# One pool for each PSUM bank, and a new order of the steps behind the attention of layer 0, in a two-layer float32 network

## The chip, the cores and the metric

The kernel runs on one core of one Trainium2 chip. The metric is the device time of one execution in microseconds (us): the median of several executions. All arithmetic is in float32; the score matmuls take their operands as pairs of rounded and residual parts.

## What is computed

The input is two images of 256 channels and 64 x 64 pixels. Cut to what matters here, the reference is:

```
# layer 0: attention over all 4096 pixels, 8 heads of 32 channels
xn  = group_norm(x)                       # groups of 8 channels
q, k, v = 1x1 convolutions of xn, with bias
x1  = x + softmax(q.T k / sqrt(32)) v

# layer 1, on n = group_norm(x1)
q, k, v = 1x1 convolutions of n           # w1, w2, w3
ctx   = attention among the 64 pixels of equal place in their 8 x 8 blocks
feats = relu(scale * (lr @ ctx) + shift)
qx, kx = two (1x1 convolution, relu) steps each of feats     # fq1 fq2, fk1 fk2
ctx2  = attention inside each 8 x 8 block; values fv @ feats
att   = relu(scale * (srw @ ctx2) + shift)
conv  = 3x3 grouped convolution of nine mixtures of q, k, v
out   = x1 + rate1 * att + rate2 * conv
```

Normalisation in layer 1 needs the mean and the variance of x1 for each group, and so every output of layer 0.

## The kernel before, in words

Channels are two chunks of 128 partitions (index k), pixels eight tiles of 512 (index t). The two images (index b) are worked one after the other, each in four stages, and each stage has its own division of PSUM, which has eight banks of 512 float32 per partition.

1. *Projections of layer 0* (project0, L408), pool ps0_b of eight banks. Each tile of q and k is evicted twice, by ACT (rounded part, L421) and DVE (residual, L422). For image 0, fold_scores (L196) makes products of the weights of layer 1 that turn its first attention into a product with one matrix g.
2. *Attention of layer 0* (attention0, L473), pool sc_b: a ring of seven banks in one tile for scores (L504), and one bank for the sums of values, av (L577). TensorE writes scores into the ring (L545), ACT takes Exp from it into a ring of 28 tiles in SBUF named es and v (L551), TensorE multiplies these with the values (L560), and DVE and DMA add them for the softmax denominators. Sixteen groups of heads and pixels are worked so. The denominators ("rows") of all but the last group go through DRAM. For the last group they are summed by TensorE into one bank of the ring, in two halves (sum_rows, L621), ahead of the last three blocks of values.
3. *First attention of layer 1* (layer1_first, L1147), pool ps1_b of eight banks. to_groups (L1154) normalises a tile into the tile xg, regrouped by place in the block. project (L1172) multiplies with g (tile py), then come the small attentions, one for each t (group_attention, L1047), whose last product pc_lr ACT evicts into feats (L1142).
4. *Second attention and convolution* (layer1_second, L1284): four banks for the convolution (pacc_b) and a pool ps2_b of four for the rest.

Between 2 and 3 stands finish_last (L660): it takes reciprocals of the rows (L674), copies the rows for a later check (kept, L680 for image 0 and L683 for image 1), multiplies the sums with the reciprocals, adds bias and input (L685), takes statistics of the result (L687 to L691), and gives back put, which copies the last 32 channels into the x tiles (L695), one copy for each of four tiles. At the start of stage 3 follow, for the second chunk, statistics over groups (Stats: means, spread, variances, deviations), with two tiny matmuls (pm_l, pv_l).

In stage 3, image 0 also has fold_products (L249). It transposes w3 and fv (tiles pt_w and pt_fv, copied by ACT at L259), and multiplies them with lr and srw (pm_w and pm_fv, copied at L267), so that two products of the network become one. It is a generator: each next(fold) issues one step, between steps of to_groups.

**What sets the order.** The framework records instructions and a planner orders those of each engine by simulated readiness. Inside tc.manual_schedule the named engines keep the written order: TensorE, ACT and DVE in attention0 and at the start of layer1_first (L1212), TensorE alone later. ACT and DVE work of stage 4, and in the kernel before the POOL work of stage 3, is ordered by the planner, which may also let the tail of one hand-ordered part overlap the head of the next. A tile of a pool that follows another pool in the same place waits until the tiles it covers are released. Accesses to one bank of one tile are kept in order across engines, unless tc.declare_no_dep says otherwise. xg is in the same place of SBUF as most of the ring es (pool apool, tag A), so that nothing may be written to xg before the last matmul has read es.

In the kernel before, the eight tiles of to_groups for the first chunk go to POOL (t = 5, 6, 7) and to ACT (the rest), and those of the second chunk to ACT (two for image 0, three for image 1) and DVE.

## Time and profile before

| what | us |
|---|---|
| median of 3 executions (3056.49 to 3058.67) | 3057.96 |
| the profiled execution, its own time | 3062.01 |
| its span, from the first to the last instruction | 3060.1 |
| TensorE (PE) busy in the span | 2979.3 |
| VectorE (DVE) busy | 2455.9 |
| ScalarE (ACT) busy | 2340.2 |
| GpSimd (POOL) busy | 832.1 |

The stages of image 0 meet at about 113 us (projections to attention), 1136 us (attention to layer 1) and 1248 us (first to second attention of layer 1); those of image 1 at about 1637, 2662 and 2764 us. The mean granted TensorE clock was 0.991.

A profile row names line, engine, operation, tile written <- tiles read, shapes, count, then busy time in us, mean duration in ns, and the engine's idle time before these instructions with what ended it. PEld is the loading of weights into TensorE. In the list of waits, a row is the waiting engine and line, the releasing one, the total in us, how often, and the longest. Buffer numbers and what follows them are cut from names: xg_0 is xg, pm_l1_0 is pm_l, wt_w3 is wt_w.

### The profile page before, as it was taken

The numbers are of one execution on the slowest core, as the hardware profiler recorded it, in microseconds if no ns is written. First come the engines' busy times: TensorE is split into PE (matmuls) and PEld (weight loads), VectorE is DVE, ScalarE is ACT, GpSimd is POOL, SyncE is SP. The second block draws the span as 40 slices with busy tenths as digits, with TensorE's granted clock in tenths as the row PEclk, the third lists the DMA queues.
The fourth block names the chain that finished last, engine by engine and source line by source line (L and its number), as shares of the span: only waits on it lengthen the run. The fifth ranks groups of instructions, "written<-read, shape, count | busy, mean of one in ns | idle before, by whom it ended". The sixth has DMA issues, their size and how long they took to land. (4 is left out here: it accounts for less than half of the span.)

```text
span 3060.1 us, 63941 instructions
## 1 busy us (share of the span) xinstructions
PE 2979.3 (97%) x25129; PEld 1859.9 (61%) x25129; DVE 2455.9 (80%) x3122; ACT 2340.2 (76%) x3266; POOL 832.1 (27%) x918
## 2 busy tenths in 40 slices
PE   7999999999999999999989999999999999999998
PEld 4565556655556556577755555666555565576765
DVE  4598998989899999856556989989988899835543
ACT  2699999999999984623237999999999999834333
POOL 1022222322223230155301222222222222306440
PEclk9999999999999999999999999999999999999999
DMA  7978789787897661230159787797878976700000
GB/s 259 274 137 180 150 163 175 153 172 157 176 181 159 140 135 42 73 131 28 42 193 274 134 169 163 159 181 146 174 162 167 183 160 131 170 5 4 21 15 22
DMA packets 244149, 425.01 MB, mean 139 GB/s; under 512 B 98889, under 2 KB 109949, under 8 KB 241661
## 3 DMA queue, kind: packets, MB, share of 16 engines
q0 software_dynamic: 94720, 237.57, 40.2%
q1 hardware_dynamic: 148972, 182.99, 21.6%
q8 instruction: 199, 3.26, 0.4%
q14 instruction: 114, 0.93, 0.1%
q10 hardware_dynamic: 144, 0.26, 0.0%
HBM read 119.55 MB, written 68.39 MB: 61 GB/s over the span
## 5 line engine op out<-in xcount | busy, mean ns | idle before, releaser
L551 ACT ACTIVATE es<-ring 128x512 f32<-128x512 f32 (+2 forms) x1572 | 1203.1, 904 | 29.9 <-PE ring L545 21.7
L545 PE MATMUL ring<-q,k 128*128 128x512 f32 x4096 | 1081.8, 407 | 11.2 <-ACT v L551 4.9
L597 DVE TENSOR_TENSOR e<-e,es 128x1024 f32<-128x1024 f32 (+1 forms) x956 | 1036.2, 1148 | 22.5 <-ACT es L551 22.2
L545 PEld LDWEIGHTS ring<-q,k 128*128 128x128 f32 x4096 | 733.4, 188 | 379.7 <-ACT es L551 115.7
L551 ACT ACTIVATE v<-ring 128x512 f32<-128x512 f32 (+2 forms) x1024 | 780.4, 899 | 23.8 <-PE ring L545 13.4
L560 PE MATMUL av<-es,v 128*32 128x256 f32 (+1 forms) x9684 | 725.2, 389 | 0.0
L597 DVE TENSOR_TENSOR e<-e,v 128x1024 f32<-128x1024 f32 (+1 forms) x636 | 670.1, 1112 | 22.4 <-ACT v L551 21.5
L560 PE MATMUL av<-v 128*32 128x256 f32 (+1 forms) x6188 | 498.0, 389 | 0.0
L560 PEld LDWEIGHTS av<-es,v 128*32 128x32 f32 x9684 | 328.3, 109 | 265.3 <-issue 105.5
L560 PEld LDWEIGHTS av<-v 128*32 128x32 f32 x6188 | 221.2, 109 | 171.2 <-issue 72.8
L996 PE MATMUL mm<-v,wf 128*128 128x256 f32 x1024 | 227.6, 380 | 1.5 <-DVE z L1005 1.5
L607 POOL DMA_DIRECT2D es<-es x118 | 100.7, 853 | 461.6 <-ACT es L551 411.4
L996 PEld LDWEIGHTS mm<-v,wf 128*128 128x128 f32 x1024 | 193.3, 190 | 36.8 <-issue 9.8
L986 POOL TENSOR_TENSOR v<-col 128x512 f32<-128x512 f32 x128 | 165.7, 1319 | 178.4 <-ACT rk_sr L1142 38.7
L1001 ACT COPY z<-mm 128x512 f32<-128x512 f32 x32 | 18.7, 586 | 183.3 <-PE mm L996 183.3
L607 POOL DMA_DIRECT2D acc<-es x118 | 119.5, 1018 | 113.8 <-ACT v L551 35.2
L605 POOL DMA_DIRECT2D es<-es x20 | 11.4, 569 | 495.2 <-ACT es L551 404.6
L607 POOL DMA_DIRECT2D es<-v x72 | 61.3, 852 | 290.8 <-ACT v L551 287.2
L1002 DVE TENSOR_TENSOR z<-z,mm 128x512 f32<-128x512 f32 x32 | 22.0, 687 | 140.1 <-ACT z L1001 139.7
L607 POOL DMA_DIRECT2D v<-es x112 | 114.3, 1020 | 17.7 <-ACT es L551 8.4
L607 POOL DMA_DIRECT2D acc<-v x78 | 75.1, 963 | 76.0 <-ACT es L551 31.1
L982 POOL TENSOR_TENSOR col<-xp 128x1152 f32<-128x1152 f32 x32 | 69.6, 2174 | 66.5 <-DVE xp L1420 55.1
(254 smaller groups left out, 2665.5 us busy)
## 6 DMA issues: line engine op xcount, KB each, us to landing
acc<-es POOLq DMA_DIRECT2D x128, 512.0 KB, 6.4
acc<-v POOLq DMA_DIRECT2D x84, 512.0 KB, 6.2
es<-es POOLq DMA_DIRECT2D x138, 256.0 KB, 4.3
v<-es POOLq DMA_DIRECT2D x132, 256.0 KB, 5.1
k<-wk_halves SPq DMA_DIRECT2D x64, 512.0 KB
q<-wq_halves SPq DMA_DIRECT2D x256, 128.0 KB
v<-v POOLq DMA_DIRECT2D x90, 256.0 KB, 5.0
es<-v POOLq DMA_DIRECT2D x84, 256.0 KB, 3.9
```

Of the source, the lines that this page charges most:

```text
L545: touch(nc.tensor.matmul(sc[:, i, :], held["k", g // 2][:, j * P : (j + 1) * P], held["q", g, u // 2][:, u % 2, :], start=True, stop=True, ...
L551: nc.scalar.activation(dst, sc, AF.Exp, scale=SC0), set(range(at % BANKS, at % BANKS + m))
L560: note(nc.tensor.matmul(dst[HD0 * u : HD0 * u + HD0, n], lhs, rhs(u)[:, n], start=start, stop=stop))
L597: nc.vector.tensor_add(dst[:, s, :], dst[:, s, :], src)
L605: nc.gpsimd.dma_start(out=dst, in_=src)
L607: nc.gpsimd.dma_start(out=dst, in_=src, accum_op=ALU.add)
L982: (nc.gpsimd.tensor_add if plus else nc.gpsimd.tensor_sub)(col, cols(one), cols(two))
L986: (nc.gpsimd.tensor_add if plus else nc.gpsimd.tensor_sub)(dst, rows(one), rows(two))
L996: nc.tensor.matmul(mm[:, m, r, :], wf[:, k, 4 * r + q, m * P : (m + 1) * P], v[r // 2][:, r % 2, k, :], start=k == 0, stop=k == KC - 1,)
L1001: nc.scalar.copy(z[:, 1], mm[:, :, 1, :])
L1002: nc.vector.tensor_add(z[:, 0], z[:, 1], mm[:, :, 0, :])
```

## The change

There are five parts.

1. *Banks.* Instead of one pool with four or eight buffers, open_banks opens one pool for each bank; bank() hands them out in strict turn, or one by number. av gets a pool of its own. Named banks: the second g product of fold_scores and the last q tile of image 1 take bank 7; the last pc_lr tiles take banks 2 and 3.
2. *Rows of the last group.* The two halves lie in two banks of the ring. The reciprocal and the kept copy are made half by half, with no dependence on the matmuls of the other half. For image 0, DVE multiplies the sums straight from PSUM; the ACT copy of them is gone.
3. *Folds.* Both transposes come first and then the four products, one step each.
4. *to_groups* walks its tile in the order of the input: reads have step 1, stores have step 64 elements (256 bytes) in runs of eight; before, it was reads of step 8 and stores of step 1 in runs of eight.
5. *Order of stage 3.* POOL is ordered by hand too. First chunk: image 0 has six tiles on ACT and two on POOL, image 1 seven on ACT and one on POOL. The copies of put are placed between POOL's tiles.

```diff
-    def bank(shape, name):
-        return psum["ps"].tile(shape, F32, tag="bank", name=name)
+    def open_banks(name, first):
+        stack = ExitStack()
+        places = range(first, 8)
+        psum.update(
+            turn=0, first=first,
+            banks={i: stack.enter_context(tc.tile_pool(name=f"{name}_{i}", bufs=1, space=PSUM)) for i in places},
+        )
+        return stack
+
+    def bank(shape, name, at=None):
+        if at is None:
+            at = psum["first"] + psum["turn"] % len(psum["banks"])
+            psum["turn"] += 1
+        return psum["banks"][at].tile(shape, F32, tag="bank", name=name)
...
-            pg = bank([P, C + AT], f"pt_g_{k}")
+            pg = bank([P, C + AT], f"pt_g_{k}", at=7 if k else None)
...
-        for name, behind in (("w3", "lr"), ("fv", "srw")):
-            turned = w4([P, KC, C], "turned_" + name)
+        turned = {}
+        for name in ("w3", "fv"):
+            turned[name] = w4([P, KC, C], "turned_" + name)
             for j in range(KC):
...
-                nc.scalar.copy(turned[:, j, :], pt)
+                nc.scalar.copy(turned[name][:, j, :], pt)
             yield
+        for name, behind in (("w3", "lr"), ("fv", "srw")):
             for k in range(KC):
...
                 nc.scalar.copy(wts[name][:, k, :], pt)
+                yield
             nc.sync.dma_start(out=kept_w[name], in_=wts[name])
-            yield
...
-                pq = bank([P, T], f"p_{nt}")
+                final = b > 0 and (nm, g, t) == ("wq0", KC - 1, NT - 1)
+                pq = bank([P, T], f"p_{nt}", at=7 if final else None)
...
-                sums[g] = psum["sc"].tile([P, T], F32, tag="av", name=f"av_{b}_{g}")
+                sums[g] = psum["av"].tile([P, T], F32, tag="av", name=f"av_{b}_{g}")
...
                 for part in range(2):
+                    at, note = rows[part], rows_made[part].append
                     for j in SUMMED_LAST:
-                        quarters(rows, ones, lambda u: unit(g, j, u), j == SUMMED_LAST[0], False, part)
+                        quarters(ring[:, at, :], ones, lambda u: unit(g, j, u), j == SUMMED_LAST[0], False, part, note)
...
-            for part in range(2):
-                n = slice(part * T // 2, (part + 1) * T // 2)
-                nc.vector.reciprocal(avs[:, 1, n], rows[:, n])
             kept = w4([P, T], f"kept_{b}")
             y = avs[:, 0, :]
-            if b == 0:
-
-                nc.scalar.copy(y, sums[g])
-                nc.scalar.copy(kept, rows)
-                nc.vector.tensor_mul(y, y, avs[:, 1, :])
-            else:
-                nc.scalar.copy(kept, rows)
-                nc.vector.tensor_mul(y, sums[g], avs[:, 1, :])
+            for part, at in enumerate(rows):
+                n = slice(part * T // 2, (part + 1) * T // 2)
+                for made in (nc.vector.reciprocal(avs[:, 1, n], ring[:, at, n]), nc.scalar.copy(kept[:, n], ring[:, at, n])):
+                    for other in rows_made[1 - part]:
+                        tc.declare_no_dep(made.ins, other.ins, reason="another bank of the ring")
+            nc.vector.tensor_mul(y, sums[g], avs[:, 1, :])
...
-                    held["rows"] = spare_bank()
+                    held["rows"] = []
+                    for _ in range(2):
+                        spare_bank()
+                        held["rows"].append(spare[0])
...
-            pc = bank([P, T], f"pc_{nm}_{m}")
+            pc = bank([P, T], f"pc_{nm}_{m}", at=ends and ends[m])
...
-            dst = xg[:, k, :, t, :].rearrange("p (d e) o -> p d e o", d=8)
-            src = xts[t][:, k, :].rearrange("p (d o e) -> p d e o", d=8, o=8)
+            dst = xg[:, k, :, t, :].rearrange("p (d e) o -> p d o e", d=8)
+            src = xts[t][:, k, :].rearrange("p (d o e) -> p d o e", d=8, o=8)
...
-        with tc.manual_schedule(engines={E.PE, E.Activation, E.DVE}):
+        with tc.manual_schedule(engines={E.PE, E.Activation, E.DVE, E.Pool}):
             st.aggregate(second)
             fold = fold_products() if b == 0 else iter(())
-            put(nc.gpsimd.tensor_copy, (0, 1))
-            for t in range(5, NT):
-                to_groups(0, t, nc.gpsimd)
-            pm, pv = bank([P, 1], f"pm_l1_{b}"), bank([P, 1], f"pv_l1_{b}")
-            for t in range(3):
-                to_groups(0, t, nc.scalar)
+            n_pool = 2 - b
+            by_act = iter(range(NT - n_pool))
+            for half in range(2):
+                if half < n_pool:
+                    to_groups(0, NT - 1 - half, nc.gpsimd)
+                put(nc.gpsimd.tensor_copy, (2 * half, 2 * half + 1))
+            if b == 0:
+                to_groups(0, next(by_act), nc.scalar)
+            next(fold, None)
+            next(fold, None)
+            if b:
+                for t in by_act:
+                    to_groups(0, t, nc.scalar)
+            for _ in range(2):
+                for t in (next(by_act, None),):
+                    if t is not None:
+                        to_groups(0, t, nc.scalar)
                 next(fold, None)
-            to_groups(0, 3, nc.scalar)
-            if b:
-                to_groups(0, 4, nc.scalar)
-            next(fold, None)
-            st.means(second, pm, nc.vector.tensor_copy)
+            st.means(second, bank([P, 1], f"pm_l1_{b}"), nc.vector.tensor_copy)
             st.spread(second)
             firsts = [lambda t=t, m=m: project(t, m, slice(0, 1)) for t in range(3) for m in range(KC)]
             if b:
                 firsts.pop(0)()
+            else:
+                to_groups(0, next(by_act), nc.scalar)
             next(fold, None)
-            st.variances(second, pv)
+            st.variances(second, pv := bank([P, 1], f"pv_l1_{b}"))
             st.deviations(second, pv)
             shift_of(st, 1)
-            if b == 0:
-                to_groups(0, 4, nc.scalar)
-            put(nc.gpsimd.tensor_copy, (2, 3))
+            for t in by_act:
+                to_groups(0, t, nc.scalar)
             n_act = 2 + b
...
+                        ends=(2, 3) if t == NT - 1 else None,
...
-        with tc.tile_pool(name=f"ps0_{b}", bufs=8, space=PSUM) as psum["ps"]:
+        with open_banks(f"ps0_{b}", 0):
...
-        with tc.tile_pool(name=f"sc_{b}", bufs=1, space=PSUM) as psum["sc"]:
+        with (
+            tc.tile_pool(name=f"sc_{b}", bufs=1, space=PSUM) as psum["sc"],
+            tc.tile_pool(name=f"av_{b}", bufs=1, space=PSUM) as psum["av"],
+        ):
             put, check, st = attention0(b, xts, held)
-        with tc.tile_pool(name=f"ps1_{b}", bufs=8, space=PSUM) as psum["ps"]:
+        with open_banks(f"ps1_{b}", 0):
             between = layer1_first(b, xts, put, check, st)
         with (
             tc.tile_pool(name=f"pacc_{b}", bufs=1, space=PSUM) as pacc,
-            tc.tile_pool(name=f"ps2_{b}", bufs=4, space=PSUM) as psum["ps"],
+            open_banks(f"ps2_{b}", 4),
         ):
```

More of the change, by code (lines that the diff above doesn't have):

```diff
@@ L264, in fold_products @@
                     nc.tensor.matmul(
-                        pt, turned[:, j, k * P : (k + 1) * P], outer[behind][:, j, :], start=j == 0, stop=j == KC - 1
+                        pt, turned[name][:, j, k * P : (k + 1) * P], outer[behind][:, j, :],
+                        start=j == 0, stop=j == KC - 1,
                     )
                 nc.scalar.copy(wts[name][:, k, :], pt)
+                yield
             nc.sync.dma_start(out=kept_w[name], in_=wts[name])
-            yield
         pt = bank([P, KC], "pb_lr")
@@ L503, in attention0 @@
         recent, spare = [], [0]
+        rows_made = ([], [])
         ring = psum["sc"].tile([P, BANKS, T], F32, tag="ring", name=f"ring_{b}")
@@ L623, in sum_rows @@
                 for part in range(2):
+                    at, note = rows[part], rows_made[part].append
                     for j in SUMMED_LAST:
-                        quarters(rows, ones, lambda u: unit(g, j, u), j == SUMMED_LAST[0], False, part)
-                    quarters(rows, ones, lambda u: acc[u], False, False, part)
-                    quarters(rows, ones, lambda u: added[g][u // 2][:, u % 2, :], False, True, part)
+                        quarters(ring[:, at, :], ones, lambda u: unit(g, j, u), j == SUMMED_LAST[0], False, part, note)
+                    quarters(ring[:, at, :], ones, lambda u: acc[u], False, False, part, note)
+                    quarters(ring[:, at, :], ones, lambda u: added[g][u // 2][:, u % 2, :], False, True, part, note)
                 return
@@ L1045, in direct_layers, with group_attention @@
     SC1 = C ** -0.5
-    def group_attention(nm, q, k, tokens, wv, out, busy=False, apart=False, more=None, between=None):
+    def group_attention(nm, q, k, tokens, wv, out, busy=False, apart=False, more=None, between=None, ends=None):
         vs = w4([P, 4, C], f"vs_{nm}")
```

## The prediction

> **What bounds the kernel now.** First the page's busy shares:
>
> ```profile
> PE 2979.3 (97%) x25129; PEld 1859.9 (61%) x25129; DVE 2455.9 (80%) x3122; ACT 2340.2 (76%) x3266; POOL 832.1 (27%) x918
> ```
>
> TensorE is busy for 2979.3 of 3060.1 us, so no edit that leaves its matmuls alone can return more than its idle time of 81 us, plus what a lowered clock costs after an idle stretch. The diff adds and removes no matmul. So I read next for whom TensorE waits, and keep the rows that the diff can reach:
>
> ```profile
> PE phq_sr L1354 <- ACT feats L1142: 4.1, 2, 2.8
> PE py L1181 <- POOL xg L1161: 2.2, 1, 2.2
> PE py L1181 <- ACT xg L1158: 1.6, 1, 1.6
> PE pt_w L258 <- ACT kept L680: 1.6, 1, 1.6
> PE ring L545 <- DVE hl_wq L422: 1.6, 1, 1.6
> PE ring L545 <- ACT w_at L236: 0.5, 1, 0.5
> ```
>
> Together 11.6 us; they lie at the seams between PSUM pools. The largest row of that view (26.0 us, of which 19.2 at the start) is mostly loading and statistics, which stay. Third, the order of time behind layer 0, image 0 (start, duration, engine, line, idle before):
>
> ```profile
> 1135.41 1.32 ACT L1158 ACTIVATE xg<-x,shift,rstd_l 128x512 f32<-128x512 f32 x1 [5.86 <-PE av L560]
> 1135.44 7.69 POOL L1161 TENSOR_SCALAR xg<-x,mean_l,rstd_l 128x512 f32<-128x512 f32 x3 [12.13 <-PE av L560]
> 1137.74 0.66 PE L258 MATMUL pt_w<-ident,wt_w 128*128 128x128 f32 x4 [1.57 <-ACT kept L680]
> 1149.35 10.52 PE L1181 MATMUL py<-xg,wt_g 128*128 128x512 f32 x20 [1.64 <-ACT xg L1158]
> ```
>
> The xg tile takes the place of the es ring, so ACT and POOL may begin only when the last AV matmul has read es (1135.4), whatever their order. From there to 1149.35 TensorE does only folds and tiny statistics: that stretch is set by ACT. Fourth, image 1, in 2 us stretches (PE, PEld, DVE, ACT, POOL busy, then the clock):
>
> ```profile
> 2664.00:2666.00 2.00, 0.00 (x0) 0.00 (x0) 1.89 (x6) 2.00 (x3) 2.00 (x1) 0.82 0.94 354
> 2668.00:2670.00 2.00, 0.53 (x1) 0.50 (x2) 0.43 (x3) 0.00 (x0) 1.94 (x2) 0.50 1.03 422
> ```
>
> TensorE stands still, its clock falls to half, and POOL is what it waits for. Fifth, what one such operation costs by shape (busy, mean ns):
>
> ```profile
> L1158 ACT ACTIVATE xg<-x,shift,rstd_l 128x512 f32<-128x512 f32 x15 | 19.0, 1313 | 12.1 <-PE av L560 11.7 <-DVE shift L361 0.4
> L1161 POOL TENSOR_SCALAR xg<-x,mean_l,rstd_l 128x512 f32<-128x512 f32 x6 | 15.8, 2645 | 23.9 <-PE av L560 23.9
> L1300 ACT ACTIVATE xp<-x,shift,rstd_l 128x512 f32<-128x512 f32 x29 | 21.7, 809 | 1.1 <-PE pvs_lr L1060 1.1
> L1142 ACT ACTIVATE feats<-pc_lr,vecs 128x512 f32<-128x512 f32 x32 | 36.5, 1232 | 6.6 <-PE pc_lr L1129 6.6
> L1142 ACT ACTIVATE hq_sr<-phq_sr,vecs 128x512 f32<-128x512 f32 x32 | 24.8, 777 | 16.8 <-PE phq_sr L1354 15.7 <-ACT xp L1300 0.9 <-issue 0.2
> ```
>
> The same 512 elements take ACT 0.81 us in a straight walk, 1.31 us when it reads every eighth element (L1158), 1.23 us when it stores at every 64th (feats). Last, the entry to the score ring of image 1:
>
> ```profile
> 1637.70 1.28 ACT L551 ACT_TABLE_LOAD   x1
> 1638.52 2.35 PE L545 MATMUL ring<-q,k 128*128 128x512 f32 x9 [1.56 <-DVE hl_wq L422]
> 1639.05 7.50 ACT L551 ACTIVATE es<-ring 128x512 f32<-128x512 f32 x9
> ```
>
> **What the skill says.** "TensorE: Matmul & The Clock Gate", Part 1, has the array fall to half rate after a largely idle window of about 3.4 us and return after a busy one. The trace agrees: 0.50 in the stretch above, and two halved stretches in image 0 (about 1139.8 to 1142.5 and 1149.9 to 1153.4). Idle of 2.3 us cost clock, of 1.8 us did not. "PSUM — Partial Sum Buffer", section on bank collisions, wants readers on ACT and DVE of one bank kept apart, reads too; the trace has the kept copy only after both reciprocals of the same bank (1137.10 after 1137.01). "ScalarE: Activation LUTs", What ACT_TABLE_LOAD costs, prices an ACTIVATE at 186 ns plus 0.833 ns an element plus 93 ns for each pointer operand, 0.80 us here; L1300 agrees, L1158 lies 0.5 above. "GPSIMD Engine Reference", section 7, makes reads with steps over 8 bytes half again as dear; L1161 on POOL reads with 32-byte steps and takes 2.65 us; no run shows it with straight reads.
>
> **The walk of to_groups.** It now reads straight and stores at every 64th element. On ACT: 0.80 plus what feats pays over hq (1.232 - 0.777 = 0.455) gives 1.25 us against 1.31, and with the usual 0.1 us overlap one each 1.15 us against 1.20. Below, 0.80 if short runs of eight escape the penalty; above, no row bounds it. I take 1.25. On POOL 1.3 to 2.65, I take 2.6 (no gain). On DVE (now 744 ns) 0.55 to 1.2, I take 0.74; its tiles are needed only after six first-half projections, so this hides.
>
> **Banks at the score ring.** The last tile in bank 7 frees banks 0 to 6 earlier, and both ring waits (0.5 and 1.6) can go. But ACT still evicts that tile, loads the Exp table until 1638.98 and only then reads the ring (1639.05 now). TensorE fills seven banks and waits there: I book -0.1 in all; all 2.1 if the planner moved the table load, 0 at worst.
>
> **Seam of image 0.** Each half of the row sums has a bank, so the first reciprocal need not wait for the second half: DVE is free at 1132.8 and started at 1133.64, 0.84 lost. Two reciprocals then end at 1136.2, the second kept copy (about 0.4) at 1136.7 to 1137.0. The ring is one tile, so folds still wait for that copy: TensorE starts about 1137.0, not 1137.74, and gains 0.7 of the 1.57. All four transposing copies now precede the products, so transposes of fv hide the copies of w3, and the 0.3 and 1.1 us fold waits close. The ACT copy of sums (0.57) goes; DVE's multiply reads PSUM in the same 0.69. ACT now carries, to the end of the first half of xg: six to_groups (6.9 + 0.1), eight fold copies less one pair after it (about 7 x 0.27), sqrt 0.26, the kept copy 0.3, some 0.6 of waiting for transposes: 10.1 us from 1135.41, so 1145.5, and TensorE starts py at 1145.65, not 1149.35: -3.7. POOL: one to_groups to 1138.0, the put that waits for y (about 1138), 1.2, the next to 1141.9, put to 1143.2; behind these stand only the DMA issues of conv weights, now at 1143.1, so no loss. SP's store of a folded weight moves by a step and nobody waits. TensorE ends its folds at about 1143.6, so 2 us idle remain; with tiny matmuls before it the clock falls about every second time. Now py takes 10.52 us where 20 pieces of 0.43 make 8.6: 1.9 at stake. I take half: -4.7 together (-3.8 cold, -5.6 warm). DVE's second-half tiles and conv weights move up with it, else the weights' reload, with 3 to 5 us in hand before their transposes at 1306, would be late next.
>
> **Seam of image 1.** Seven to_groups on ACT: 7 x 1.15 + 0.1 + 0.3 for the kept copy from 2661.25 end at 2669.7. POOL ended at 2669.41 now. The wait on POOL becomes a wait on ACT: +0.35. The statistics arrive 0.8 earlier and wait behind it.
>
> **Named banks at the last lr tile.** phq's first products need only feats[0]; the pool made them wait for feats[1], which reads the last bank. With banks 2 and 3 they run at once, and up to 1.33 and 1.7 us of idle close. But ACT, with images ahead of it (six xp in image 1, until 2771.30), evicts phq at 2771.86: with that order kept only 0.3 and 0.56 remain, else 1.3 and 1.4. I take 0.8 and 1.0: -1.8.
>
> **Turns elsewhere.** In the second stage each tile reuses the bank of four tiles before. The closest case is the score bank, read by DVE until 1290.36, wanted at 1292.15: 0.
>
> **Sum.** -0.1 - 4.7 + 0.35 - 1.8 = -6.25, on a profiled execution of 3062.0 (span 3060.1 and 1.9 around it), which lies 4 us above the median. Against the median 3057.96: 3051.7.
>
> **Rivals.** (a) ACT stores runs of eight at its straight rate, 0.80 us. Then image 0 is bound by folds: py from 1143.65, warm, ends at 1152.3 against 1159.87, -7.6; image 1: 2661.25 + 7 x 0.7 + 0.4 = 2666.5, -2.9; total -12.4, 3045.5. For it: straight stores in runs of eight cost nothing (res, 778 ns). Against: feats. (b) The waits don't go: pools still join over whole tiles and the planner keeps ACT's order: only order gains, about -2, 3056. For it: the ring stays one tile. (c) Slower: the strided store on ACT. Each 0.1 us a tile adds 0.6 in image 0 and 0.7 in image 1. The gain is used up at 1.73 us a tile; at 2.6, what POOL pays today for the awkward walk, 3057.96 - 6.25 + 13.5 x 1.3 = 3069. Against: feats shows 1.23 for the same stride.
>
> **Chances.** Main case 44% (3047 to 3055 by its ends: faster 0.29, same 0.15), (a) 34%, all faster, (b) 10% (0.03, 0.06, slower 0.01), (c) 12% (same 0.01, slower 0.11). A measurement of this kernel tells about 0.2% from no change, 6.1 us. Faster 0.66, same 0.22, slower 0.12. The range reaches to (a) and (b) and leaves out (c): 3043 to 3057.
>
> **What would show it.** Right: pt_w starts within 1 us of the last AV matmul; L1158 at 1.2 to 1.3 us; py of image 1 waits for ACT; ring waits gone but the first Exp no earlier after its table load; phq starts before feats[1] ends. Wrong: L1158 at 0.8 or over 1.7; the kept copy still last at the seam; new TensorE waits in the second stage.

## The result

The changed kernel took **3054.77 us** (median of 22 runs, 3051.24 to 3059.21). The kernel before took 3061.16 us (22 runs beside it on the same chip). The ratio is **0.9982, 95% interval 0.9976 to 0.9988**, so the change is worth 5.5 us by the ratio (3.7 to 7.3) and 6.4 us between the medians. A second set of 18 runs gave 3054.76 us and a ratio of 0.9979 (0.9972 to 0.9986). The forecast was 6.25 us less. Its absolute time, 3051.7 us, came out 3.1 us low, since it started from the 3057.96 us of three executions, and 22 give 3061.16. The size of the gain is right, but its parts are not: three terms fell short, two brought more, and they cancel.

The profiled execution of the changed kernel took 3055.84 us, with a span of 3053.6 (before 3062.01 and 3060.1). Below, L1174 and L1177 are to_groups on ACT and on POOL or DVE, L694 the reciprocals and kept copies, L1197 py, L271 the transposing folds, L1158 the bn_relu evictions (feats, hq_sr), L1325 the image tiles xp.

The marks on TensorE, in the order of work: ring is a score and av a sum of values in layer 0; py is the product with g, and pa follows it and gives queries and keys; sp_lr is the score of a small attention of stage 3 (a tile of the "lr phase") and pc_lr its last product, which reads bd, a copy of the transposed attention weights. The last pc_lr is the end of the lr phase. In stage 4, phq and prq are the two convolution steps of the query branch (phq is evicted into hq_sr, which prq reads), mm is a product of the 3x3 convolution, and sp_sr and pc_sr are what sp_lr and pc_lr are in stage 3.

**Profile after, read in the order of the prediction.** The busy shares first, then the rows of TensorE's waits (total us, times, longest) that answer to the six shown of before:

```profile
PE 2975.5 (97%) x25129; PEld 1857.4 (61%) x25129; DVE 2449.6 (80%) x3122; ACT 2340.7 (77%) x3270; POOL 823.9 (27%) x915
```

```profile
PE prq_sr L1388 <- ACT hq_sr L1158: 3.0, 2, 2.8
PE py L1197 <- ACT xg L1174: 1.8, 1, 1.8
PE phq_sr L1379 <- ACT feats L1158: 1.1, 1, 1.1
PE py L1197 <- POOL xg L1177: 1.1, 1, 1.1
PE pt_w L271 <- ACT kept L694: 0.9, 1, 0.9
```

The rows of ring for hl_wq and w_at are gone. The 4.1 us of phq have shrunk to 1.1, but **a new row has come, prq for hq_sr, with the same 2.8 us in one wait**: the stall at the end of image 1's lr phase has moved on by one product.

The seam of image 0 in order of time (start, duration, engine, line, names; idle before in brackets):

```profile
1133.04 1.75 DVE L694 RECIPROCAL avs<-ring 128x256 f32<-128x256 f32 x1
1134.83 0.37 ACT L694 COPY kept<-ring 128x256 f32<-128x256 f32 x1 [4.97 <-DVE avs L694]
1135.23 1.76 DVE L694 RECIPROCAL avs<-ring 128x256 f32<-128x256 f32 x1 [0.44 <-ACT kept L694]
1137.02 0.37 ACT L694 COPY kept<-ring 128x256 f32<-128x256 f32 x1
1137.45 0.66 PE L271 MATMUL pt_w<-ident,wt_w 128*128 128x128 f32 x4 [0.95 <-ACT kept L694]
1142.50 2.51 POOL L1177 TENSOR_SCALAR xg<-x,mean_l,rstd_l 128x512 f32<-128x512 f32 x1
1143.31 4.35 ACT L1174 ACTIVATE xg<-x,shift,rstd_l 128x512 f32<-128x512 f32 x4
1145.71 2.05 PE L1197 MATMUL py<-xg,wt_g 128*128 128x512 f32 x2 [1.05 <-POOL xg L1177]
```

The last AV matmul ends at 1136.50. From there py starts 9.21 us later, where before it took 13.18: 3.97 us gained at the start of py. The first two matmuls of py take 2.05 us, not 0.86, so the clock is halved behind the idle stretch. The seam of image 1 and the costs by shape (busy, mean ns):

```profile
2658.24 5.34 ACT L1174 ACTIVATE xg<-x,shift,rstd_l 128x512 f32<-128x512 f32 x5
2663.72 2.05 PE L1197 MATMUL py<-xg,wt_g 128*128 128x512 f32 x2 [1.83 <-ACT xg L1174]
```

```profile
L1174 ACT ACTIVATE xg<-x,shift,rstd_l 128x512 f32<-128x512 f32 x18 | 20.4, 1247 | 1.5 <-PE av L577 1.1 <-DVE shift L376 0.4
L1177 DVE TENSOR_SCALAR xg<-x,mean_l,rstd_l 128x512 f32<-128x512 f32 x11 | 9.1, 980 | 0.3 <-issue 0.2
L1177 POOL TENSOR_SCALAR xg<-x,mean_l,rstd_l 128x512 f32<-128x512 f32 x3 | 7.6, 2541 | 24.9 <-PE av L577 24.8
```

ACT's 1247 ns is the 1.25 us of the forecast. But five of them in a row took 5.34 us: one every 1.02 us, not every 1.15.

**Where the time went, stage by stage.** Whether the clock is halved behind a wait differs from execution to execution of one kernel, so a difference of two single profiles misleads by 1 to 3 us in a stage. The table therefore gives the profile of before, that of the changed kernel, and the mean over the profiles of the kernels that leave the stage as it is in the changed one (in brackets how many, the changed kernel among them; pool_first below counts at the seam, since py doesn't move there, and unnamed is left out in image 0's attention and up to its first mm, where the names bear). Times in us between two marks on TensorE.

| stage | before | changed | mean (n) | mean less before | forecast |
|---|---|---|---|---|---|
| image 0, first p_wk to last AV | 1111.88 | 1112.56 | 1112.1 (12) | +0.2 | 0 |
| image 0, last AV to first py | 13.18 | 9.21 | 9.2 (9) | -4.0 | -3.8 |
| image 0, last AV to first mm of the second stage | 177.06 | 173.58 | 173.1 (6) | **-4.0** | -5.5 (seam and lr end) |
| image 0, first mm to last pc_sr | 235.81 | 233.31 | 233.7 (11) | **-2.1** | 0 |
| image 1, first p_wk to last AV | 1109.61 | 1109.91 | 1110.5 (13) | **+0.9** | -0.1 |
| image 1, last AV to first py | 7.46 | 7.13 | 7.1 (11) | -0.3 | +0.35 |
| image 1, first py to first pa | 11.98 | 10.84 | 11.6 (12) | -0.4 | 0 |
| image 1, last pc_lr to first mm | 11.76 | 12.79 | 12.3 (8) | **+0.5** | -1.0 |
| image 1, first mm to the end | 283.90 | 283.27 | 283.2 (10) | **-0.7** | 0 |

The third row contains the second. Without the second the means add up to -5.9 us, against 6.4 and 7.2 between the medians of the two sets. There is one profile of before to subtract from, and where its clock happened to fall is part of these numbers: about 1.5 us of the -2.1, all of the -0.4, and 0.4 of the +0.9, as shown below. Without that the means show about 4.4 us, and the remainder isn't accounted for.

### The profile page after: what moved, and what is told of

Its sections match the earlier page's. It is cut to its first block, busy times and chain, and to the rows that moved or that the text cites. A ratio compares the mean times of both kernels' runs of the same rounds, so it can differ in the third digit from the quotient of the medians.

```text
span 3053.6 us, 63947 instructions
## 1 busy us (share of the span) xinstructions
PE 2975.5 (97%) x25129; PEld 1857.4 (61%) x25129; DVE 2449.6 (80%) x3122; ACT 2340.7 (77%) x3270; POOL 823.9 (27%) x915
## 4 chain that ended last, share of the span: by engine, by line
PE 89%; DVE 4%; ACT 3%; DMA 3%; issue 2%; SPq 0%; POOL 0%; ACTq 0%; DVEq 0%; POOLq 0%
PE ring L562 32%; PE av L577 29%; PE mm L1012 7%; PE p_wk L432 2%; PE pv L455 2%; PE p_wq L432 2%; PE prq_sr L1388 2%; PE prk_sr L1388 2%; PE pvs_sr L1076 2%; PE pvs_lr L1076 2%; PE py L1197 2%; PE phk_sr L1379 2%; PE phq_sr L1379 2%; DMA acc<-v 1%; PE pc_sr L1145 1%
```

## The experiments

Twelve kernels ran in three groups, each beside the kernel before on one chip. This is what they took; the medians of before were 3060.5 to 3062.0 us, so a difference of 1 us between groups says little. All their intervals overlap that of the changed kernel, those of seam_old, prep_third, images_late and best by little: the stages in the profiles carry the findings, and the totals agree with them. All five runs of images_late (3051.92 at most) lie below all 18 of changed_again (3052.13 at least) on the same chip.

| kernel | median us (runs) | ratio to before, 95% interval | against 3054.8 |
|---|---|---|---|
| walk_old | 3055.86 (21) | 0.9986 (0.9980 to 0.9993) | +1.1 |
| stage4_pool | 3057.02 (21) | 0.9990 (0.9984 to 0.9997) | +2.3 |
| unnamed | 3057.21 (13) | 0.9991 (0.9982 to 0.9999) | +2.4 |
| seam_old | 3058.06 (14) | 0.9995 (0.9987 to 1.0003) | +3.3 |
| image_dve | 3054.92 (11) | 0.9982 (0.9973 to 0.9991) | +0.2 |
| pool_first | 3054.95 (16) | 0.9981 (0.9974 to 0.9989) | +0.2 |
| all_three | 3054.83 (14) | 0.9975 (0.9967 to 0.9983) | +0.1 |
| prep_third | 3051.49 (6) | 0.9966 (0.9954 to 0.9978) | -3.3 |
| changed_again | 3054.76 (18) | 0.9979 (0.9972 to 0.9986) | 0 |
| images_late | 3051.14 (5) | 0.9966 (0.9952 to 0.9979) | -3.6 |
| bd_act | 3052.72 (8) | 0.9972 (0.9961 to 0.9982) | -2.0 |
| best | 3050.01 (5) | 0.9965 (0.9951 to 0.9979) | -4.8 |

The theory after the result: the seam of image 0 is ACT's and gained as forecast, but DVE takes part of it back in the lr phase; the named banks brought nothing, since ACT's queue stands behind them; and the second stage gained by an order that the separate pools let the planner choose. The rival for each: it is the clock, which happened to fall otherwise in the two profiles.

### Undoing the walk: walk_old

```diff
-            dst = xg[:, k, :, t, :].rearrange("p (d e) o -> p d o e", d=8)
-            src = xts[t][:, k, :].rearrange("p (d o e) -> p d o e", d=8, o=8)
+            dst = xg[:, k, :, t, :].rearrange("p (d e) o -> p d e o", d=8)
+            src = xts[t][:, k, :].rearrange("p (d o e) -> p d e o", d=8, o=8)
```

> The changed kernel with the old walk in to_groups (strided read, straight store) on all three engines, the rest as changed. Theory: ACT's to_groups go from 1.25 to 1.31 us, and, back to back, from 1.02 to 1.20 us a tile. At the seam of image 1 seven of them follow one another, so py starts 1.2 to 1.3 us later after the last AV matmul; at the seam of image 0 py waits for POOL, ACT's 0.3 to 0.7 later at most reach the 0.4 us that ACT has in hand there, so 0 to 0.5. DVE's to_groups fall from 980 to about 745 ns, with no gain. In all 1.3 to 1.8 us more than the changed kernel, 3056 to 3057. Rival: the walk is worth nothing and the seam of image 1 gained by its order alone: py starts as in the changed kernel, 3055. Second rival: DVE's slower store is what the first tiles behind image 0's seam gave back: then the stretch from pa to the last pc_lr of image 0 is 1 us shorter with the old walk, and the total is about 3055.

Measured: py of image 1 starts 8.14 us behind the last AV, not 7.13, and py of image 0 9.75, not 9.21; 3055.86 us in all. The row of ACT in image 1's seam, and the costs by shape:

```profile
2660.29 6.09 ACT L1174 ACTIVATE xg<-x,shift,rstd_l 128x512 f32<-128x512 f32 x5
```

```profile
L1174 ACT ACTIVATE xg<-x,shift,rstd_l 128x512 f32<-128x512 f32 x18 | 22.7, 1327 | 1.5 <-PE av L577 1.1 <-DVE shift L376 0.4
L1177 DVE TENSOR_SCALAR xg<-x,mean_l,rstd_l 128x512 f32<-128x512 f32 x11 | 8.3, 818 | 0.3
L1177 POOL TENSOR_SCALAR xg<-x,mean_l,rstd_l 128x512 f32<-128x512 f32 x3 | 8.0, 2677 | 23.7 <-PE av L577 23.6
```

Five tiles take 6.09 us where the new walk took 5.34: 0.15 us a tile, although one operation is only 0.08 longer. The theory held, a little below its size (1.0 us at image 1's seam where 1.2 to 1.3 was expected). On DVE the new walk is the dearer one: image 1's five take 0.82 to 0.85 us, here 0.73 to 0.75, without effect on the end. On POOL the walk is worth nothing: image 0's first to_groups takes 2.58 us with either, and the two means differ by the tile that runs beside DVE (2.88 us here, 2.51 in the changed kernel). The second rival, that DVE's slower store is what the lr phase gives back, isn't borne out: mm of image 0 comes 173.39 us behind the last AV here and 173.1 with the new walk.

### Undoing the second stage's pools: stage4_pool

```diff
-            open_banks(f"ps2_{b}", 4),
+            tc.tile_pool(name=f"ps2_{b}", bufs=4, space=PSUM) as psum["one"],
...
+        if psum.get("one") is not None:
+            return psum["one"].tile(shape, F32, tag="bank", name=name)
```

> The changed kernel with the second stage's four banks back in one pool that hands them out; all other banks as changed. Theory: with a pool for each bank the planner could put the first two products of the next tile's q branch between the first two and the last six pc matmuls of a tile, where they fill the time in which the second eviction of the values is awaited; with the one pool it can't, and each tile from the third on costs 0.15 to 0.2 us more: 12 tiles, 1.8 to 2.4 us, so about 3057. Tile to tile in the second stage of image 1: 34.78 us, not 34.65. Rival: the 2.5 us that the second stage of image 0 lost came from where the halved clock happens to fall, and the order is worth nothing: 3055, spacing 34.65 in both.

Measured: 3057.02 us, 2.3 more. TensorE's order at the same place, the changed kernel first, then this one, then before (start, duration):

```profile
2837.99 0.68 PE L1145 MATMUL pc_sr<-bd,vs_sr 128*128 128x128 f32 x4
2838.51 1.02 PE L1379 MATMUL phq_sr<-feats,wt_fq 128*128 128x512 f32 x2
2839.38 1.39 PE L1145 MATMUL pc_sr<-bd,vs_sr 128*128 128x128 f32 x11
```

```profile
2838.57 2.23 PE L1147 MATMUL pc_sr<-bd,vs_sr 128*128 128x128 f32 x16
2840.64 1.02 PE L1381 MATMUL phq_sr<-feats,wt_fq 128*128 128x512 f32 x2
```

```profile
2844.05 2.23 PE L1129 MATMUL pc_sr<-bd,vs_sr 128*128 128x128 f32 x16
2846.11 1.02 PE L1354 MATMUL phq_sr<-feats,wt_fq 128*128 128x512 f32 x2
```

With the one pool the order of before returns, and with it its spacing to the hundredth: from tile to tile 41.69, 41.69, 43.75 in image 0 (changed 41.49, 41.51, 43.55) and 34.89, 34.78, 34.78, 34.78 in image 1 (34.78, 34.65, 34.57, 34.63). In sum over the tiles that is 0.6 us in image 0 and, with the way from the last tile to the end (0.26 us), 0.8 in image 1: 1.4 of the 2.3 measured. Nothing else in TensorE's order differs. So the order is shown as a cause; the rest of the 2.1 us in image 0 is a stretch behind a 2.50 us wait, where before ran at half clock (tile to tile 46.96, changed 45.03, other kernels 45.0 to 46.6). That part is the rival's.

### Undoing the names: unnamed

```diff
-            pg = bank([P, C + AT], f"pt_g_{k}", at=7 if k else None)
+            pg = bank([P, C + AT], f"pt_g_{k}", at=None)
...
-                pq = bank([P, T], f"p_{nt}", at=7 if final else None)
+                pq = bank([P, T], f"p_{nt}", at=None)
...
-                        ends=(2, 3) if t == NT - 1 else None,
+                        ends=None,
```

> The changed kernel with no bank named: every tile takes the next in turn (the last projection tile, the second product of the pt_g fold, the last lr tile). Theory: the waits of ring for hl_wq and w_at return (0.5 and 1.6 us), but the first AV matmul, which waits for the Exp table, starts at the same time in both; at the end of the lr phase phq waits 1.3 and 2.8 us for the second feats again, but in image 1 prq, which waits for ACT's six image tiles, starts at the same time, so only image 0 pays: 0.4 to 0.8 us more, 3055 to 3056. Rival (the sum of the prediction): 0.8 and 1.0 at the two lr ends and 0.1 at the ring: 1.9 us more, 3056.7.

Measured: 3057.21 us, 2.4 more. The profile contradicts both accounts in part. In image 1 neither the wait for hl_wq at the ring nor the longer wait of phq comes back (phq waits 1.1 us): pools of their own are enough there, names or not. In image 0 phq waits 1.33 us again, so it starts 1.54 us later behind the last pc_lr than in the changed kernel. But prq starts only 0.4 us later (5.1 us behind the last pc_lr, and 4.7 in the changed kernel and in ten others), and mm too (64.8 against 64.4): of what the names bring at phq, hq_sr's turn on ACT leaves 0.4 us, the low end of the theory. At the ring of image 0 the wait for w_at is back (0.5 us), but so is the full clock, and the first AV follows the first Exp by 5.73 us, not 6.32. There the name costs as much as it brings. The stages add up to no loss, while the runs show one whose interval (0.9982 to 0.9999) overlaps that of the changed kernel. Where it would lie is open.

### Undoing the order behind layer 0: seam_old

```diff
-                    for _ in range(2):
-                        spare_bank()
-                        held["rows"].append(spare[0])
+                    held["rows"] = spare_bank()
...
-            n_pool = 2 - b
-            by_act = iter(range(NT - n_pool))
...
+            for t in range(5, NT):
+                to_groups(0, t, nc.gpsimd)
```

> The changed kernel with the order behind layer 0 as before: row sums of the last group in one bank with one kept copy, the ACT copy of the sums in image 0, folds one after the other, five to_groups on ACT and three on POOL; the new walk, the pools and the named banks stay. Theory: the order is what the seam of image 0 gained: from the last AV to pa 23.6 us again, not 19.4, so 3.5 to 4.3 us more; the seam of image 1 waits for POOL's three again, 0.5 to 1.5 more. In all 4 to 5.8 us, 3059 to 3060.5. Rival: the new walk on ACT carries most of it, and the order alone gives 1 to 2 us: 3056 to 3057.

Measured: 3058.06 us, 3.3 more: below the theory's 4 to 5.8, above the rival's 1 to 2. From the last AV to pa it takes 21.65 us, where the theory had 23.6. py of image 0 starts 11.20 us behind the last AV: of the 3.97 us between before and changed the order has 2.0, and the new walk with the old order (and the new pools) the other 2.0 (13.18 to 11.20), so the rival's walk had at most half of it. With the new order the walk is worth 0.54 (walk_old). At the seam of image 1 the order is worth nothing: 7.17 us, against 7.13. The loss at py isn't there at mm, though: 173.72 us behind the last AV, 0.6 more than the changed kernels' mean. This profiled run took 3055.57 us and is the sixth shortest of 14 (median 3058.06), so it doesn't show what the longer ones lose.

### Is it POOL that py waits for: pool_first

```diff
-            for half in range(2):
-                if half < n_pool:
-                    to_groups(0, NT - 1 - half, nc.gpsimd)
+            for half in range(n_pool):
+                to_groups(0, NT - 1 - half, nc.gpsimd)
+            for half in range(2):
                 put(nc.gpsimd.tensor_copy, (2 * half, 2 * half + 1))
```

> The changed kernel, but POOL does both its to_groups of image 0 ahead of the first put and of the weight loads that stand between. Theory: py of image 0 waits for POOL's second to_groups, which ends 6.7 us behind its first only because four DMA issues and the put stand between; done first it ends at 4.5 us behind the last AV, and py waits for ACT, 8.2 to 8.3 us behind the last AV and not 9.2: 0.9 to 1.0 us. Of that nothing is left at the first mm of the second stage, since at the last lr tiles PE waits for DVE, which has the conv weights ahead of it: mm 173.5 us behind the last AV as in the changed kernel, total 3055. Rival: the 0.9 us stay: 172.6, total 3054.

Both the theory and the rival fell. py starts 9.22 us behind the last AV, as ever:

```profile
1135.55 5.20 POOL L1177 TENSOR_SCALAR xg<-x,mean_l,rstd_l 128x512 f32<-128x512 f32 x2 [12.67 <-PE av L577]
1143.10 4.41 ACT L1174 ACTIVATE xg<-x,shift,rstd_l 128x512 f32<-128x512 f32 x4
1143.49 3.73 POOL L708 COPY x<-avs 32x512 f32<-32x512 f32 x4
1145.50 1.96 PE L1197 MATMUL py<-xg,wt_g 128*128 128x512 f32 x4 [1.74 <-POOL x L708]
```

POOL is done with xg at 1140.75, and the profile names another POOL row, which py doesn't read. What py does need is ACT's sixth tile, the second of the four in the row of ACT. It ends at 1145.40 here and at 1145.61 in the changed kernel, and py follows 0.10 us later both times. **The releaser printed beside py was the wrong one**; the forecast's bound was right, ACT's sixth tile at 1145.5 and py 0.15 us behind it. Since py didn't move, what would be left at mm of a gain there went untested.

### The second channel of two image tiles to DVE, and the reciprocals: image_dve, all_three

```diff
-                    to_image(tt)
+                    to_image(tt, b > 0 and t == 0)
```

> The changed kernel, but at the start of image 1's second stage the second channel half of two image tiles (3 and 4) is normalised on DVE and not on ACT. Theory: six image tiles, 0.72 us apart, stand on ACT ahead of the eviction hq_sr, and that is what takes back the gain of phq's earlier start. With two fewer hq_sr ends 1.4 us earlier, prq waits 1.3 us and not 2.77, POOL's first columns start 1.4 us earlier too, mm follows, and DVE, idle there for 22 us, hides its two tiles (0.53 us each): 1.4 us less than the changed kernel, 3053.4. Rival: mm waits for POOL's columns and not for prq: prq 1.4 us earlier, mm unmoved, 3055.

No gain: 3054.92 us. The planner filled ACT's two free places with later image tiles, so six xp (each one channel chunk of an image tile) still stand between feats and hq_sr. prq waits 2.06 us, not 2.77, and DVE's two tiles lie ahead of the last bd, whose wait rises from 1.04 to 1.46 us. all_three has this edit and that of pool_first, and a third, which declares away the waits between DVE's and ACT's work on different banks of the row sums:

```diff
+            taken += [(nc.scalar.copy(kept[:, n], ring[:, at, n]), part) for part, (n, at) in enumerate(zip(halves, rows))]
...
+                for other in rows_made[1 - part] + [o for o, p in taken if p != part and (o in taken_by_dve) != (made in taken_by_dve)]:
+                    tc.declare_no_dep(made.ins, other.ins, reason="another bank of the ring")
```

> The two edits above together, and a third: the two reciprocals of the row sums, and the two kept copies, keep their order on each engine but no longer wait for the other engine's work on the other bank. Theory: the second reciprocal starts as the first ends, 0.44 us earlier, and pt_w 0.4 to 0.5 us earlier; py of image 0 still waits for ACT, 8.2 us behind the last AV. In all the 1.4 us of the image tiles, 3053.4, if the lr phase of image 0 takes the rest back; 3052.0 if it doesn't. Rival: the second kept copy was set by ACT's to_groups, not by the reciprocal: pt_w unmoved, 0.95 us behind the last AV.

Measured: 3054.83 us. The second reciprocal starts at 1134.56 as the first ends, and y, the multiply, begins 0.54 us sooner behind the last AV. But pt_w gains only 0.17 us (0.78 behind the last AV, not 0.95): the kept copy now waits its turn behind ACT's first to_groups. The rival had it.

### What takes the seam's gain back: prep_third, bd_act

```diff
-                for i in range(12):
+                for i in range(4):
                     src, s = wx[:, i, :], weff[:, m, i, tap : tap + 1]
```

> The changed kernel with DVE's building of the conv weights cut down: each sum takes four of its twelve terms, so 144 of the multiply-adds of image 0's lr phase are left out and the output differs. Theory: at image 0's last lr tiles PE waits 1.9 and 2.1 us for DVE (bd), where image 1, which builds no weights, waits 1.0 us once; these multiply-adds in DVE's queue are the cause, and also what takes the seam's gain back. Without them the waits fall to about 1 us, the first mm comes 170.5 to 171.5 us behind the last AV and not 173.5, in all 2 to 3 us less: 3052 to 3053. Rival: the last tile's chain of score, exponential and transposes is simply long when no next tile fills it, whatever else DVE does: the waits stay, 173.5, 3055.

```diff
-            nc.vector.tensor_copy(
-                bd[rows, :, tt, :].rearrange("p (a u) i -> p u a i", a=2), at[rows]
-            )
+            copy = nc.scalar.copy if more and tt else nc.vector.tensor_copy
+            copy(bd[rows, :, tt, :].rearrange("p (a u) i -> p u a i", a=2), at[rows])
```

> The changed kernel, but in the lr stages the second of the two copies that build bd (0.42 us each on DVE) goes to ACT, which is half idle there. Theory: at image 0's last lr tiles PE waits for DVE; each wait loses 0.4 us by the parallel copy, and DVE carries 3.4 us less ahead of them: 0.8 to 2 us at the first mm of image 0 (171.5 to 172.8 us behind the last AV and not 173.5), and 0.4 at image 1's last lr tile (bd wait 0.6 and not 1.04). In all 1.2 to 2.4 us less, 3052.5 to 3053.8. Rival: the planner fills DVE's free places with conv weights again, so image 0 gains nothing, only 0.4 in image 1; or the copy waits on ACT behind feats and loses: 3055.

The last two lr tiles of image 0: the changed kernel, then prep_third (its last tile; the one before it doesn't wait), then bd_act:

```profile
1236.44 2.96 PE L1145 MATMUL pc_lr<-bd,vs_lr 128*128 128x128 f32 x16 [1.86 <-DVE bd L1136]
1241.95 3.76 PE L1145 MATMUL pc_lr<-bd,vs_lr 128*128 128x128 f32 x16 [2.09 <-DVE bd L1136]
```

```profile
1238.21 2.02 PE L1145 MATMUL pc_lr<-bd,vs_lr 128*128 128x128 f32 x16 [1.04 <-DVE bd L1136]
```

```profile
1234.82 2.05 PE L1144 MATMUL pc_lr<-bd,vs_lr 128*128 128x128 f32 x16 [0.28 <-ACT bd L1137]
1240.16 2.97 PE L1144 MATMUL pc_lr<-bd,vs_lr 128*128 128x128 f32 x16 [2.66 <-ACT bd L1137]
```

Without two thirds of the weights' multiply-adds the last wait falls to image 1's 1.04, the last tiles run at full clock (16 products in 2.02 us, not 2.96 and 3.76), and mm comes 169.77 us behind the last AV, 3.3 us less than the changed kernels' mean; the total falls by 3.3 us. With one bd copy on ACT mm comes at 170.67, 2.4 us less, by the first of the two waits above all (1.86 to 0.28 us): the last one is now on ACT and no shorter (2.66 us). In image 0 both theories held at mm, and the rival that the chain is simply long fell: DVE's queue is what the lr phase of image 0 ends on. But the waits there are as long in before (1.63 and 2.34 us), so the change didn't bring them. That they take back what py gains is argued: before wasn't run with the smaller weights. A second place of the same kind is the wait of the score for keys, which DVE writes: it is 1.05 to 1.55 us in the four kernels with the changed seam where py ran at full clock, and 0.13 or less where it was halved, so a full clock at py keeps little of its 1.4 us. In image 1 bd_act lost: the copy stood on ACT behind feats, the wait rose from 1.04 to 2.14 us, and mm comes 0.5 us later behind pa than where prq runs at full clock. Hence 2.0 us in all.

### Once more, and ACT's queue ahead of hq_sr: changed_again, images_late

> The changed kernel once more, beside the three below, to see which stages of a profile repeat. Theory: what the waits set repeats within 0.1 us (py of image 0 9.2 us and py of image 1 7.1 us behind the last AV, phq of image 1 1.1 us and prq 7.6 us behind the last pc_lr); what differs by 1 to 3 us is whether the clock is halved in the stretch behind a wait (py to pa in image 1: 10.8 or 12.0; prq to mm in image 1: 5.2 or 3.5). Total 3054 to 3055.5.

The waits repeat: py of image 0 at 9.24, py of image 1 at 7.12, phq at 1.08, prq at 7.55 us. The clock doesn't: from prq to mm 6.55 us here, 5.23 in the first profile, 3.54 in others.

```diff
                 for tt in images.get(t, ()):
-                    to_image(tt)
+                    with tc.issue_after(kept["hid"].ins):
+                        to_image(tt)
```

(In image 1 only; hid is the last hq_sr of the tile.)

> The changed kernel, but in image 1's second stage ACT may take the image tiles from the fourth on only after the evictions hq_sr of the tile at hand. Theory: six image tiles, 0.72 us apart, stand ahead of hq_sr on ACT and are what took back phq's earlier start; behind it they have 20 us and more. Then hq_sr follows phq, prq starts 5.5 to 6.2 us behind the last pc_lr and not 7.6, and the first mm 9.0 to 9.8 us behind it and not 11.1 (clock full in both), as POOL needs the first three image tiles alone: 1.3 to 2 us less, 3053. Rival: mm waits for POOL's columns (2.1 us, then 1.3 us for each of the first two v), which start no earlier: mm stays at 11.1, 3055.

The start of image 1's second stage, the changed kernel first:

```profile
2758.67 3.70 PE L1379 MATMUL phq_sr<-feats,wt_fq 128*128 128x512 f32 x8 [1.09 <-ACT feats L1158]
2760.11 4.31 ACT L1325 ACTIVATE xp<-x,shift,rstd_l 128x512 f32<-128x512 f32 x6
2764.31 1.44 ACT L1158 ACTIVATE hq_sr<-phq_sr,vecs 128x512 f32<-128x512 f32 x2
2765.14 5.40 PE L1388 MATMUL prq_sr<-hq_sr,wt_fq 128*128 128x512 f32 x8 [2.77 <-ACT hq_sr L1158]
2770.38 0.81 PE L1012 MATMUL mm<-v,wf 128*128 128x256 f32 x3
```

```profile
2759.36 3.70 PE L1379 MATMUL phq_sr<-feats,wt_fq 128*128 128x512 f32 x8 [0.41 <-ACT feats L1158]
2760.10 2.19 ACT L1325 ACTIVATE xp<-x,shift,rstd_l 128x512 f32<-128x512 f32 x3
2762.25 1.70 ACT L1158 ACTIVATE hq_sr<-phq_sr,vecs 128x512 f32<-128x512 f32 x2
2763.08 3.70 PE L1388 MATMUL prq_sr<-hq_sr,wt_fq 128*128 128x512 f32 x8
2766.61 1.67 PE L1012 MATMUL mm<-v,wf 128*128 128x256 f32 x7
```

Six xp ahead of hq_sr become three, prq no longer waits, its clock stays full (3.70, not 5.40 us), and mm comes 7.66 us behind the last pc_lr, where the changed kernel needs 11.1 with a full clock and 12.8 to 14.1 with a halved one. The total falls by 3.6 us, twice what was expected of the edit. So the queue on ACT is shown to be what took back the gain of phq's earlier start.

### Together: best

images_late, bd_act and the reciprocals of all_three in one kernel.

> The changed kernel with the late image tiles, the bd copy on ACT and the two reciprocals that no longer wait for the kept copy. Theory: the gains of the first two add up with 0.2 us of the third, 2.7 to 4.6 us less than the changed kernel: 3050.5 to 3052. Rival: the image tiles that are held back meet the bd copies or the feats evictions on ACT, and one gain eats the other: 3053.5.

Measured: 3050.01 us, ratio 0.9965 (0.9951 to 0.9979): faster than both kernels, 4.8 us below the changed one, but less than the sum. mm of image 0 comes 174.0 us behind the last AV, where bd_act had 170.7. py starts 1.8 us later and pa another 1.2, since py waits:

```profile
1141.56 4.93 POOL L1178 TENSOR_SCALAR xg<-x,mean_l,rstd_l 128x512 f32<-128x512 f32 x1
1142.89 2.71 DVE L1178 TENSOR_SCALAR xg<-x,mean_l,rstd_l 128x512 f32<-128x512 f32 x4
1146.55 2.07 PE L1198 MATMUL py<-xg,wt_g 128*128 128x512 f32 x2 [3.49 <-POOL xg L1178]
```

POOL's second to_groups takes 4.93 us beside four of DVE's; in the changed kernel, where the two overlap by 1.0 us, it took 2.51 and DVE's first gave way instead (1.49 us). It costs 1.8 us at py. bd_act, which has in image 0 all of this but the reciprocals' edit, starts py at 9.21, so the earlier statistics are the suspect, and no more: images_late and bd_act without that edit wasn't run.

## Why the prediction was right, and where it wasn't

**The walk of to_groups** (1.25 us on ACT, 1.15 apart; POOL and DVE unchanged). Right for one operation, 1247 ns, and rivals (a) and (c) fell with it. The spacing was mis-sized: 1.02 us. The usual overlap of 0.1 us, taken from the old walk, doesn't hold for the new one: it is 0.23. On POOL "no gain" was right (2.58 us either way). On DVE 0.74 us was forecast and 0.83 measured (image 1), with no effect on the end.

**Banks at the ring** (-0.1). Both waits went, as said, and the first Exp followed its table load as before. But a loss took their place in both images. In image 1 of the changed kernel, first ACT's order, then stretches of 2 us (PE, PEld, DVE, ACT, POOL busy, then the clock), and last the stretch of before that answers to the second:

```profile
1632.55 1.28 ACT L568 ACT_TABLE_LOAD   x1
1633.85 7.50 ACT L568 ACTIVATE es<-ring 128x512 f32<-128x512 f32 x9
```

```profile
1634.00:1636.00 2.00, 0.98 (x2) 0.37 (x2) 0.00 (x0) 2.00 (x3) 0.00 (x0) 1.00 1.03 377
1638.00:1640.00 2.00, 2.00 (x6) 1.19 (x4) 2.00 (x3) 2.00 (x4) 0.00 (x0) 0.50 1.03 296
```

```profile
1642.00:1644.00 2.00, 1.82 (x8) 0.80 (x6) 1.57 (x2) 2.00 (x4) 0.00 (x0) 1.00 1.01 302
```

TensorE fills the ring, stands still for the Exp (0.96 and then 0.85 us) and finds its clock halved at 1638 to 1640, where before had 1.00 throughout. From the start of the first Exp to the first AV it takes 6.32 us, before 5.73; image 0 has the same two numbers within 0.01, and unnamed, where image 0 keeps the old wait, has 5.73 there. So in image 0 these 0.6 us are shown to be the price of the earlier start; in image 1 no kernel brings the old wait back, and the same pattern stands for it. Why the clock falls there is open: in before TensorE stands still for longer at this place (1.56, 0.66 and 0.18 us) and keeps it. From image 1's first p_wk to its last AV the changed kernels' mean is 0.9 us longer; the rest is the rival's, the clock: behind the first p_wk it is halved for 3.55 us in before and for 3.9 to 5.1 in the others, and the way to the Exp is longer by half the difference. The step "TensorE fills seven banks and waits there" was right and its price, the clock, was left out: the prediction had read an idle time of 1.8 us as harmless.

**Seam of image 0** (-4.7, py at 1145.65). py starts at 1145.71 and waits for ACT's sixth tile, as forecast. The last AV ended at 1136.50 here and at 1136.17 in before, so counted from it 9.48 us were forecast and 9.21 measured. One inner step failed: the second reciprocal didn't end at 1136.2 but at 1136.99 (0.46 us late, counted from the last AV), since it waited 0.44 us for the first kept copy. The prediction freed the reciprocal from the second half of the sums but not from the other engine's read of the same tile, though of another bank. pt_w lost 0.1 us by it (0.95 behind the last AV, forecast 0.83), because the kept copy has its turn behind ACT's first to_groups; py, which ACT sets, didn't feel it. "I take half" for the clock had no count behind it (in before the clock fell at both seams), but it fits: in nine profiles with this seam py ran at full clock in four (8.75 us from py to pa) and not in five (10.1 to 10.5). What failed is the end of the step: the gain was counted as if it lasted. Of the 4.0 us at py 3.6 are left at the last pc_lr, which waits for DVE, and what a full clock brings at py is lost again in the wait for keys. With 0.4 us of the named banks, 4.0 arrive at mm, of 5.5 forecast (4.7 and 0.8).

**Seam of image 1** (+0.35). The wait did become one on ACT, as said. Its size has the wrong sign because of the spacing: seven tiles at 1.02 and not 1.15 us make up 0.9 us, more than the 0.65 between the forecast and the -0.3 measured. The statistics, forecast 0.8 us earlier, were not (pm_l starts 4.74 us behind the last AV, in before 4.66), but py doesn't wait for them.

**Named banks** (-1.8, by half). The prediction named the obstacle, ACT's six image tiles ahead of the eviction of phq, and the two ends, 0.3 and 0.56 with that order kept. The order was kept. It then took the middle; the low end was what happened, and in image 1 less. In image 0 0.4 us are left at prq. In image 1 the wait moved from phq (2.77) to prq (2.77), one of the new waits in the second stage that the prediction had named as a sign of being wrong. Where the clock stays full this gains 0.7 us (11.76 to 11.09 from the last pc_lr to mm), but in four of eight profiles prq runs at half clock and 1.0 to 2.4 us are lost: +0.5 on average, where -1.0 was forecast.

**Turns elsewhere** (0). Wrong: this is where the missing gain was found. The prediction asked only whether a bank was awaited, and answered rightly that none is. It didn't ask what the planner would do with banks that it may choose freely: 1.4 us in the order's spacing, 2.3 by the runs of stage4_pool.

**Sum.** Against -6.25: ring +0.9, image 0 to mm -4.0, image 1's seam with py -0.7, its lr end +0.5, second stage -2.8, image 0's attention +0.2, in all -5.9 from profiles, and -5.5 to -6.4 from runs. The parts erred by about 4 us each way, so that the number came out right was luck.

## What to carry to other kernels

A wait that is removed is worth what the next engine in line lets through: read which queue stands behind it (ACT's image tiles, DVE's weights) before booking it, and look for the order that frees that queue; here this (images_late, 3.6 us) was worth more than half of what the whole change brought. When an allocation is loosened, compare the order of the instructions before and after, since a planner uses freedom that no wait had shown. And if a stall can halve the clock, compare stages over several profiles, not over two.

## What was not expected of the hardware

- ACT overlaps strided stores more than strided reads: to_groups of 1.25 us come every 1.02 us, those of 1.33 us every 1.20 (five in 5.34 and 6.09 us).
- DVE pays for the strided store, 0.83 us for 128x512 against 0.74 with the strided read; POOL takes 2.58 us either way (image 0's first tile).
- POOL and DVE at work on to_groups at the same time: in best POOL took 4.93 us, in the changed kernel 2.51 and DVE's first 1.49 us, where DVE's last, with POOL done, took 0.82. Which of the two gives way differs, and the runs don't show what decides it.
- One stall of 2.77 us on TensorE was followed by full clock in four of eight profiles of the same stretch and by a halved one in the other four: 3.54 us from prq to mm, or 5.2 to 6.6. In image 1 two stalls of 0.96 and 0.85 us at the ring had a halved clock behind them in all 13 profiles with this start, while before, with stalls of 1.56, 0.66 and 0.18 us at the same place, kept the full one.
- In the clock records of before and of the changed kernel a halved stretch within the span lasts 3.41 us or a multiple of it (6.83, 10.24, 13.65). One such stretch over busy matmuls costs 1.7 us: 10.45 against 8.75 from py to pa, 5.23 against 3.54 from prq to mm.
